# Turning attention probabilities on VectorE and by DMA instead of on TensorE

## The chip, the cores and the metric

The kernel runs on one core of a Trainium2 chip. The metric is the device time of one execution in microseconds. The core has five engines with their own instruction streams: TensorE (PE in the profile; its weight loads are PEld), VectorE (DVE), ScalarE (ACT), GpSimd (POOL) and SyncE (SP), which here only issues DMAs. Each stream runs in order, and the streams wait for each other by semaphores. Matmul results land in PSUM, everything else is in SBUF, 128 partitions wide.

## The reference

Two layers on x (8 batches x 256 tokens x 256 features, float32) with a context of 256 tokens x 192 features:

```python
x = x + xattn0(layernorm(x), ctx, mask, ...)       # 16 heads of 16
x = x + soft_moe(layernorm(x), ...)                # 8 experts, 128 slots each
x = x + xattn1(layernorm(x), ctx, ...)             # 16 heads of 64: the second attention
x = x + channel_mix(layernorm(x), ...)
```

The second attention, which alone is changed, is

```python
q = (x @ w_q).reshape(B, SQ, 16, 64)
k = (cond @ w_k).reshape(B, SKV, 16, 64)
v = (cond @ w_v).reshape(B, SKV, 16, 64)
attn = softmax(einsum('bqhd,bkhd->bhqk', q, k) * 64 ** -0.5, axis=-1)
out = einsum('bhqk,bkhd->bqhd', attn, v).reshape(B, SQ, 1024)
return out @ w_out + b_out
```

The softmax runs along the keys, so the probabilities come out with queries on the partitions. The product with v sums over keys, so it wants keys on the partitions: between the two the probabilities must be transposed.

## The kernel before

The kernel is one program in four parts; the third is the second attention. It handles 8 batches. A *step* is two of the 16 heads of one batch (t = 0 to 7), and `steps1` gives each step as a list of stages:

- stage 0, `scores`: four matmuls (L73 is the helper that records them) put the scores of two heads and 256 queries into a PSUM tile `sc` (two buffers, tag `big`). VectorE takes the row maxima `nm` (L1201). ScalarE takes four exponentials with their sums into `ex` and `z` (L1206).
- stage 1, `norm`: VectorE takes `rz`, the reciprocal of the sums (L1217); GpSimd multiplies the 128x1024 probabilities by it (L1219).
- stage 2, `transposes`: TensorE transposes the probabilities in eight 128x128 blocks (L76) into two PSUM tiles `pe` (tag `mm`, three buffers, shared with the projections); VectorE and ScalarE copy one each to `et` (L1235).
- stage 3, `values`: eight matmuls with `V` and `et` into `o`, and after every second step a ScalarE copy to `ot` (L1254).
- stage 4, `project` (after the last step of a batch): sixteen matmuls with the output weights into `po`, and VectorE adds the result to x (L1267).

Beside the steps stand the projections of later batches: `xt_piece` (normalised x, transposed: `xT`, L1121), `q_piece` (into `q`, scaled into `QT` by VectorE, L1141), `keys` (into `k`, copied to `KT` by ScalarE and VectorE, L1106 and L1107) and `values_of` (into `v`, copied to `V`, L1171 and L1172).

Two steps make a group, and there are 32 groups, four for a batch. The loop at the end of the part (L1293) sets the order of the work: in its pass n it records stage 3 of group n-3, a q piece or `xt_piece` of the next batch, stage 4 of group n-4, stages 2 and 1 of groups n-2 and n-1, a key or value projection, and stage 0 of group n. Matmuls, transposes and `rz` keep this order on their engines (`keep_in_program_order`). The passes of one batch differ: n % 4 = 0 has `xt_piece` and no q; 1 and 2 have one q piece; 3 has two q pieces and `project`. The last projections end with pass 27. The DMAs of this part load its weights (L1067 to L1080, issued from 900 to 906 us); the next DMAs that SP issues load the weights of the fourth part (L1321).

Of the kernel before, what the change touches and what calls it, by code (L numbers as in the profile page):

```python
# [8 lines left out]
F32 = mybir.dt.float32  # L9
U8 = mybir.dt.uint8  # L10
AF = mybir.ActivationFunctionType
ALU = mybir.AluOpType
AX = mybir.AxisListType

P = 128
B, S, D, C = 8, 256, 256, 192
NT = B * S // P
H = 16
HD0, HD1 = 16, 64
# [43 lines left out]
def kernel(ctx: ExitStack, tc: tile.TileContext, a: dict, out: bass.AP):  # L63
    nc = tc.nc
# [10 lines left out]
    def transpose(out, in_):  # L75
        tc.keep_in_program_order(nc.tensor.transpose(out, in_, ident))  # L76
# [7 lines left out]
    def ps_mm(name):  # L84
        return ps.tile([P, 512], F32, tag="mm", bufs=3, name=name)
# [137 lines left out]
    with ExitStack() as l0:  # L223
# [372 lines left out]
        for p in range(1, 4):  # L596
            h, b = 16 * (p - 1), 2 * p
# [160 lines left out]
        for b, plan in enumerate(  # L758
# [8 lines left out]
            for step in plan.split():  # L767
                when, _, args = step[1:].partition(".")
# [293 lines left out]
    with ExitStack() as l1:  # L1062
# [48 lines left out]
        def proj1(b):  # L1111

            to = {}

            def xt_piece():
                mv, rstd = xat_stats[b // 2]
                pt = transposed(normed(b, mv, rstd, "l1", of=4), f"x1_{b}", transpose)
                to["xT"] = p1.tile([P, 2, S], F32, tag="xT", bufs=1, name=f"xT1_{b}")  # L1120
                nc.vector.tensor_copy(to["xT"], pt)  # L1121
                for t in range(2):
                    nc.gpsimd.tensor_tensor(
                        x_sb[:, 2 * b + t, :], x_sb[:, 2 * b + t, :], bo, ALU.add
                    )

            def q_piece(t2):
                if t2 == 0:
                    to["QT"] = p1.tile([P, 8, S], F32, tag="QT", bufs=2, name=f"QT1_{b}")
                pq = ps_mm(f"q1_{b}_{t2}").rearrange("p (t n) -> p t n", t=2)  # L1130
                for i in range(2):
                    t = 2 * t2 + i
                    for c in range(2):
                        matmul(
                            pq[:, i, :],
                            lhsT=wq[:, c, t * P : (t + 1) * P],
                            rhs=to["xT"][:, c, :],
                            start=(c == 0),
                            stop=(c == 1),
                        )  # L1140
                nc.vector.tensor_scalar(  # L1141
                    to["QT"][:, 2 * t2 : 2 * t2 + 2, :], pq, HD1**-0.5, None, ALU.mult
                )

            def values_of(u):

                if u == 0:
                    to["V"] = p1.tile([P, 2, DA], F32, tag="V", bufs=2, name=f"V1_{b}")
                pv = [ps_mm(f"v1_{b}_{u}_{h}") for h in range(2)]
                t0 = S * b + u * P  # L1150
                cols = [slice(h * 512, (h + 1) * 512) for h in range(2)]
                for h in range(2):
                    matmul(
                        pv[h],
                        lhsT=ctx0T[:, t0 : t0 + P],
                        rhs=wv[:, 0, cols[h]],
                        start=True,
                        stop=False,
                    )

                def halves():
                    for h in range(2):
                        r = slice(64 * h, 64 * h + 64)
                        matmul(
                            pv[h],
                            lhsT=ctx1T[r, t0 : t0 + P],
                            rhs=wv[r, 1, cols[h]],
                            start=False,
                            stop=True,
                        )  # L1170
                    nc.scalar.copy(to["V"][:, u, cols[0]], pv[0])  # L1171
                    nc.vector.tensor_copy(to["V"][:, u, cols[1]], pv[1])  # L1172

                return halves

            qs = [[xt_piece]] + [[lambda t=t: q_piece(t) for t in ts] for ts in ((0,), (1,), (2, 3))]
            return to, qs, [lambda u=u: values_of(u) for u in range(2)]

        def steps1(b, to):
# [4 lines left out]
            for t in range(8):  # L1184
# [3 lines left out]
                def scores(t=t, tag=tag, st=st):  # L1188
                    sc = ps_big(f"sc_{tag}").rearrange("p (h q k) -> p h q k", h=2, q=2)
                    for qb in range(2):  # L1190
                        for i in range(2):
                            r = slice(64 * i, 64 * i + 64)
                            matmul(
                                sc[:, i, qb, :],
                                lhsT=to["QT"][r, t, qb * P : (qb + 1) * P],
                                rhs=to["KT"][r, t, b % 2 * S : (b % 2 + 1) * S],
                                start=True,
                                stop=True,
                            )
                    nm = stat.tile([P, 2, 2], F32, tag="nm1", bufs=4, name=f"nm_{tag}")  # L1200
                    nc.vector.tensor_reduce(nm, sc, AX.X, ALU.max, negate=True)  # L1201
                    ex = p1.tile([P, 2, 2, S], F32, tag="ex", bufs=6, name=f"ex_{tag}")
                    z = stat.tile([P, 2, 2], F32, tag="z1", bufs=6, name=f"z_{tag}")
                    for qb in range(2):
                        for i in range(2):
                            nc.scalar.activation(  # L1206
                                ex[:, i, qb, :],
                                sc[:, i, qb, :],
                                AF.Exp,
                                bias=nm[:, i, qb : qb + 1],  # L1210
                                accum_out=z[:, i, qb : qb + 1],
                            )
                    st["ex"], st["z"] = ex, z
# [9 lines left out]
                        ALU.mult,  # L1223
                    )

                def transposes(tag=tag, st=st):
                    et = p1.tile([P, 2, 2, S], F32, tag="et", bufs=4, name=f"et_{tag}")
                    for i in range(2):
                        pt = ps_mm(f"pe_{tag}_{i}").rearrange("p (c q) -> p c q", c=2)
                        for qb in range(2):  # L1230
                            for c in range(2):
                                transpose(
                                    pt[:, c, qb * P : (qb + 1) * P],
                                    st["ex"][:, i, qb, c * P : (c + 1) * P])
                        (nc.scalar.copy if i else nc.vector.tensor_copy)(et[:, i, :, :], pt)  # L1235
                    st["et"] = et

                def values(t=t, tag=tag, st=st):
                    if t == 0:
                        blk["ot"] = p1.tile([P, 8, S], F32, tag="ot", bufs=2, name=f"ot_{tag}")  # L1240
                    if t % 2 == 0:
                        blk["o"] = ps_o(f"o_{tag}").rearrange("p (t q) -> p t q", t=2)
                    for c in range(2):
                        for i in range(2):
                            h = 2 * t + i
                            matmul(
                                blk["o"][64 * i : 64 * i + 64, t % 2, :],
                                lhsT=to["V"][:, c, h * HD1 : (h + 1) * HD1],
                                rhs=st["et"][:, i, c, :],
                                start=(c == 0),  # L1250
                                stop=(c == 1),
                            )
                    if t % 2 == 1:
                        nc.scalar.copy(blk["ot"][:, t - 1 : t + 1, :], blk["o"])  # L1254

                def project(tag=tag):
# [12 lines left out]
                    )  # L1269

                steps.append(
                    [scores, norm, transposes, values] + ([project] if t == 7 else [])
                )
            return steps

# [4 lines left out]
        def stage(k, n):  # L1280
            for step in groups[n] if 0 <= n < len(groups) else ():
                if k < len(step):
                    step[k]()
# [9 lines left out]
        for n in range(len(groups) + 4):  # L1293
            b, i = n // 4 + 1, n % 4
            stage(3, n - 3)
            if b < B:
                for piece in projs[b][1][i]:
                    piece()
            stage(4, n - 4)
            stage(2, n - 2)  # L1300
            stage(1, n - 1)


            if i < 2 and n // 8 < B // 2 - 1:
                keys(n // 8 + 1, n % 8 // 4 * 2 + i)()
            elif i >= 2 and b < B:
                projs[b][2][i - 2]()()
            stage(0, n)
            if n == 20:
                ffn_stats[0] = ln_half(0, "ffn_0")  # L1310
# [159 lines left out]
```

## Time and profile before

| | |
|---|---|
| time, three runs | median 1375.35 us (1374.36 to 1376.78) |
| profiled execution | 1375.81 us, span 1373.9 us |
| mean granted TensorE clock | 0.987 |
| TensorE matmuls | busy 1326.6 us, 97% of the span |
| VectorE, ScalarE, GpSimd | busy 42%, 42%, 14% |
| second attention, first row maximum to last residual add | from 943.42 to 1315.87 us of the span |

The profile is one execution. A line of a timeline gives the start, the length, the engine, the line of the kernel, the operation and its operands; `x16` at a PE line counts matmuls and weight loads together. The length of a matmul includes the time until its result is out, so successive starts, not lengths, tell what it holds the engine for. A line of windows gives the stretch, its length, the busy time and count of PE, PEld, DVE, ACT and POOL, the granted clock, the share of DMA and GB/s.

### The profile page before, as it was taken

To read this page: it belongs to the slowest core of one execution; us is meant where nothing else is said; L and a number is where in the kernel's file an instruction comes from. 1 tells how busy PE (TensorE), PEld (TensorE's weight loads), DVE (VectorE), ACT (ScalarE), POOL (GpSimd) and SP (SyncE) were. 2 spreads that over 40 slices of the span, in tenths; PEclk is the share of its full clock that TensorE was granted. 3 is DMA by queue.
4 is the path that set the end of the run, shared out by engine and by line. 5 is a ranking of instruction groups with operands and counts; after the bars stand their busy time and mean duration, and the time that the engine had idled before them with its cause. 6 is when DMAs were issued, how large, how long until landed. Compare 5 with 4: busy or idle time off the path is not lost.

```text
span 1373.9 us, 19006 instructions
## 1 busy us (share of the span) xinstructions
PE 1326.6 (97%) x7504; PEld 961.3 (70%) x7504; DVE 575.1 (42%) x1172; ACT 578.9 (42%) x1386; POOL 194.6 (14%) x149
## 2 busy tenths in 40 slices
PE   6899999899999999999999999999999999999988
PEld 3556655468678877778767888866667667577767
DVE  5777876523330233321333110025444544554544
ACT  1445444635342254522625222204544534554643
POOL 1000001101010000100001000013332332323514
PEclk9899999999999999999999999999999999999999
DMA  8000000023133323332323325340000000000011
GB/s 250 23 2 1 1 1 1 1 96 131 65 131 131 131 76 119 130 113 83 126 69 130 131 88 173 100 126 1 1 1 1 1 1 1 1 1 1 1 31 54
DMA packets 59112, 86.84 MB, mean 63 GB/s; under 512 B 3344, under 2 KB 49040, under 8 KB 59024
## 3 DMA queue, kind: packets, MB, share of 16 engines
q1 hardware_dynamic: 57440, 84.33, 18.8%
q10 hardware_dynamic: 1584, 1.31, 0.4%
q8 instruction: 59, 0.97, 0.3%
q14 instruction: 29, 0.24, 0.1%
HBM read 83.53 MB, written 2.10 MB: 62 GB/s over the span
## 4 chain that ended last, share of the span: by engine, by line
PE 84%; ACT 6%; DVE 4%; DMA 2%; issue 2%; POOL 1%; SPq 0%; POOLq 0%; ACTq 0%; DVEq 0%
PE ph L964 16%; PE pe L980 15%; PE sc L73 8%; PE q L73 6%; PE o L73 5%; PE po L73 5%; PE k L73 5%; PE pc L1006 4%; PE v L73 4%; PE pe L76 4%; PE ln L828 3%; PE pf L910 3%; ACT ex L1206 2%; PE pf L73 1%; ACT ex L497 1%
## 5 line engine op out<-in xcount | busy, mean ns | idle before, releaser
L972 ACT ACTIVATE ht<-ph,b 128x256 f32<-128x256 f32 x256 | 119.0, 473 | 372.1 <-PE ph L964 371.7
L964 PE MATMUL ph<-slots,w 128*128 128x256 f32 x1024 | 266.8, 384 | 1.1 <-ACT ht L972 0.4
L980 PE MATMUL pe<-w,ht 128*128 128x256 f32 x1024 | 263.3, 381 | 0.0
L964 PEld LDWEIGHTS ph<-slots,w 128*128 128x128 f32 x1024 | 182.4, 189 | 54.4 <-ACT ht L972 21.7
L980 PEld LDWEIGHTS pe<-w,ht 128*128 128x128 f32 x1024 | 192.0, 190 | 29.9 <-DVE slots L989 4.2
L1219 POOL TENSOR_TENSOR ex<-ex,rz 128x1024 f32<-128x1024 f32 x64 | 120.2, 1898 | 224.4 <-DVE rz L1217 219.8
L1206 ACT ACTIVATE ex<-sc,nm 128x256 f32<-128x256 f32 x256 | 117.2, 483 | 45.8 <-DVE nm L1201 44.6
L73 PE MATMUL sc<-KT,QT 17*128 17x256 f32 (+1 forms) x1024 | 105.5, 383 | 5.7 <-DVE NM L486 4.8
L497 ACT ACTIVATE ex<-sc 128x512 f32<-128x512 f32 x128 | 74.6, 596 | 84.4 <-PE sc L73 76.6
L486 DVE TENSOR_REDUCE NM<-sc 128x2 f32<-128x512 f32 x128 | 86.7, 687 | 33.0 <-PE sc L73 28.7
L989 DVE TENSOR_TENSOR slots<-pe,b 128x512 f32<-128x512 f32 x32 | 22.1, 692 | 185.0 <-PE pe L980 185.0
L73 PEld LDWEIGHTS sc<-KT,QT 17*128 17x128 f32 (+1 forms) x1024 | 78.0, 189 | 29.0 <-issue 13.3
L73 PE MATMUL q<-xT,wq 128*128 128x256 f32 x384 | 95.4, 396 | 0.9 <-ACT V L1171 0.9
L73 PEld LDWEIGHTS q<-xT,wq 128*128 128x128 f32 x384 | 71.3, 193 | 27.0 <-issue 13.3
L888 POOL TENSOR_TENSOR es<-es,zs 128x1024 f32<-128x1024 f32 x12 | 22.7, 1893 | 445.8 <-DVE zs L887 445.8
L1201 DVE TENSOR_REDUCE nm<-sc 128x4 f32<-128x1024 f32 x64 | 75.4, 1219 | 6.5 <-PE sc L73 2.8
L73 PE MATMUL po<-wo,ot 128*128 128x256 f32 x320 | 72.6, 382 | 0.0
L76 PE MATMUL pe<-ident,ex 128*128 128x128 f32 x512 | 69.9, 278 | 0.5 <-DVE xT L1121 0.4
L73 PEld LDWEIGHTS po<-wo,ot 128*128 128x128 f32 x320 | 60.1, 190 | 11.3 <-issue 3.6
L1235 ACT COPY et<-pe 128x512 f32<-128x512 f32 x64 | 37.0, 607 | 71.9 <-PE pe L76 71.5
L76 PEld LDWEIGHTS pe<-ident,ex 128*128 128x128 f32 x512 | 56.3, 140 | 14.0 <-issue 8.0
L73 PE MATMUL o<-et,V 128*64 128x256 f32 x512 | 62.8, 385 | 0.9 <-ACT ot L1254 0.9
(186 smaller groups left out, 1642.7 us busy)
## 6 DMA issues: line engine op xcount, KB each, us to landing
w<-in_w_dram SPq DMA_DIRECT2D x64, 1024.0 KB, 6.4
b<-in_b_dram SPq DMA_DIRECT2D x32, 128.0 KB, 6.7
out_dram<-y SPq DMA_DIRECT2D x8, 256.0 KB, 2.1
x_sb<-in_x_dram SPq DMA_DIRECT2D x3, 512.0 KB, 6.1
ctx0T<-in_ctxT_dram SPq DMA_DIRECT2D x4, 256.0 KB, 6.8
ctx1T<-in_ctxT_dram SPq DMA_DIRECT2D x8, 128.0 KB, 5.9
se<-in_slots_dram SPq DMA_DIRECT2D x1, 1024.0 KB, 6.0
wq<-in_wq_dram SPq DMA_DIRECT2D x1, 1024.0 KB, 4.9
```

The source lines that it names most:

```text
L73: tc.keep_in_program_order(nc.tensor.matmul(out, lhsT=lhsT, rhs=rhs, start=start, stop=stop))
L76: tc.keep_in_program_order(nc.tensor.transpose(out, in_, ident))
L486: nc.vector.tensor_reduce(NMs[(2 * b + t // 2) % 2][:, qb, t, HD0 + 1 + 64 * i : 64 * i + 64 : 32], sc[i][:, :, 0, :], AX.X, ALU.max, nega ...
L497: nc.scalar.activation(ex[:, 2 - 2 * i : 4 - 2 * i, :], sc[1 - i][:, :, 1, :], AF.Exp)
L828: nc.tensor.matmul(pl[:, m * 512 : (m + 1) * 512], lhsT=st["xnT"][:, c, t * P : (t + 1) * P], rhs=snT[:, c, m * 512 : (m + 1) * 512], star ...
L964: nc.tensor.matmul(ph, lhsT=c_["w1"][:, c, hc * P : (hc + 1) * P], rhs=slots[e][:, c * 256 : (c + 1) * 256], start=(c == 0), stop=(c == 1),)
L972: nc.scalar.activation(ht, ph, AF.Gelu, bias=b1[:, e, hc : hc + 1])
L980: nc.tensor.matmul(c_["pe"][:, b, :], lhsT=c_["ht"][hc][:, b * SL : (b + 1) * SL], rhs=c_["w2"][:, hc, :], start=(hc == 0), stop=(hc == HI ...
L1006: nc.tensor.matmul(pc[:, :D], lhsT=CT[:, bl, e, t * P : (t + 1) * P], rhs=eos[e][:, bl, :], start=(e == 0), stop=(e == E - 1),)
L1201: nc.vector.tensor_reduce(nm, sc, AX.X, ALU.max, negate=True)
L1206: nc.scalar.activation(ex[:, i, qb, :], sc[:, i, qb, :], AF.Exp, bias=nm[:, i, qb : qb + 1], accum_out=z[:, i, qb : qb + 1],)
L1219: nc.gpsimd.tensor_tensor(ex, ex, rz.rearrange("p h q -> p (h q)").unsqueeze(2).to_broadcast([P, 4, S]), ALU.mult,)
```

## The change

The transposes leave TensorE. Stage 2 becomes `turn`: for each step one VectorE instruction transposes the probabilities in squares of 32x32 into `tk`, and after the second step of a group sixteen DMAs, issued by SP, move the squares from one quarter of the partitions to another, from `tk` to `et`. Each DMA moves 32 partitions of 2 KB. `et` and `tk` now hold a group each (two buffers), `ex` has four buffers where it had six. The matmuls of `values` read `et` in pieces of 32 elements. The scaling of `QT` goes from VectorE to ScalarE. In the loop, stage 2 is recorded for group n-1, not n-2, after the key or value projection and just ahead of stage 0 of group n; stage 1 comes ahead of stage 4. Stage 3 stays at group n-3. On VectorE the two turns of a group stand between the copy to `KT` or `V` and the row maxima of the next group.

```diff
-                nc.vector.tensor_scalar(
-                    to["QT"][:, 2 * t2 : 2 * t2 + 2, :], pq, HD1**-0.5, None, ALU.mult
+                nc.scalar.activation(
+                    to["QT"][:, 2 * t2 : 2 * t2 + 2, :], pq, AF.Copy, scale=HD1**-0.5
                 )
...
-                    ex = p1.tile([P, 2, 2, S], F32, tag="ex", bufs=6, name=f"ex_{tag}")
+                    ex = p1.tile([P, 2, 2, S], F32, tag="ex", bufs=4, name=f"ex_{tag}")
...
-                def transposes(tag=tag, st=st):
-                    et = p1.tile([P, 2, 2, S], F32, tag="et", bufs=4, name=f"et_{tag}")
-                    for i in range(2):
-                        pt = ps_mm(f"pe_{tag}_{i}").rearrange("p (c q) -> p c q", c=2)
-                        for qb in range(2):
-                            for c in range(2):
-                                transpose(
-                                    pt[:, c, qb * P : (qb + 1) * P],
-                                    st["ex"][:, i, qb, c * P : (c + 1) * P])
-                        (nc.scalar.copy if i else nc.vector.tensor_copy)(et[:, i, :, :], pt)
-                    st["et"] = et
+                def turn(t=t, tag=tag, st=st):
+                    if t % 2 == 0:
+                        blk["tk"] = p1.tile([P, 4, 2, 8, 32], F32, tag="tk", bufs=2, name=f"tk_{tag}")
+                        blk["et"] = p1.tile(
+                            [P, 4, 2, 2, 2, 2, 32], F32, tag="et", bufs=2, name=f"et_{tag}"
+                        )
+                    tk, et = blk["tk"], blk["et"]
+                    st["et"] = et[:, :, t % 2, :, :, :, :]
+                    tc.keep_in_program_order(
+                        nc.vector.transpose(
+                            tk[:, :, t % 2, :, :].rearrange("p k m x -> p m k x"),
+                            st["ex"].rearrange("p h q (c k x) -> p (h q c) k x", c=2, k=4),
+                        )
+                    )
+                    if t % 2 == 1:
+                        for k in range(4):
+                            for a in range(4):
+                                nc.sync.dma_start(
+                                    et[32 * k : 32 * k + 32, a].rearrange(
+                                        "p s h q c x -> p (s h q c x)"
+                                    ),
+                                    tk[32 * a : 32 * a + 32, k].rearrange("p s m x -> p (s m x)"),
+                                )
...
-                                rhs=st["et"][:, i, c, :],
+                                rhs=st["et"][:, :, i, :, c, :].rearrange("p a q x -> p q a x"),
...
-                    [scores, norm, transposes, values] + ([project] if t == 7 else [])
+                    [scores, norm, turn, values] + ([project] if t == 7 else [])
...
+            stage(1, n - 1)
             stage(4, n - 4)
-            stage(2, n - 2)
-            stage(1, n - 1)
...
+            stage(2, n - 1)
             stage(0, n)
```

## The prediction

> **What bounds the kernel now.** I read first the page's engine table, then the chain of waits inside the second attention, then timelines of TensorE, VectorE, ScalarE and GpSimd over one of its batches, then the DMA issues and the clock. The page says that TensorE is the bound overall; the chain over 1000 to 1100 us says that this holds in the second attention too, 89% of it being matmuls, 12.2% the transposes of the probabilities (`pe`, L76).
>
> ```profile
> PE 1326.6 (97%) x7504; PEld 961.3 (70%) x7504; DVE 575.1 (42%) x1172; ACT 578.9 (42%) x1386; POOL 194.6 (14%) x149
> by line: PE q L73 15.0%; PE po L73 13.8%; PE v L73 12.6%; PE pe L76 12.2%; PE sc L73 12.1%; PE k L73 11.6%; PE o L73 11.3%; ACT ex L1206 6.8%; DVE nm L1201 2.5%; ACT et L1235 1.3%; issue 1.1%; ACT ot L1254 0.6%; ACTq L1206 0.0%
> ```
>
> TensorE in the heaviest quarter of a batch (start, length, then line and operands). Starts give what each phase holds TensorE for: o 1.88, two q 3.55, po 6.91, pe 2.04, v 2.78, sc 1.8.
>
> ```profile
> 1051.06 1.89 PE L73 MATMUL sc<-KT,QT 64*128 64x256 f32 x16
> 1052.88 1.95 PE L73 MATMUL o<-et,V 128*64 128x256 f32 x16
> 1054.76 3.72 PE L73 MATMUL q<-xT,wq 128*128 128x256 f32 x16
> 1058.31 7.07 PE L73 MATMUL po<-wo,ot 128*128 128x256 f32 x32
> 1065.22 2.20 PE L76 MATMUL pe<-ident,ex 128*128 128x128 f32 x16
> 1067.26 1.88 PE L73 MATMUL v<-wv,ctx0T 128*128 128x512 f32 x4
> ```
>
> I call a tick one pass of the loop, that is, the work for one group (two steps, four heads); four ticks make a batch. One tick's softmax on the other engines: two row maxima on VectorE in 2.36 us, eight exponentials on ScalarE from 1043.11 to 1046.72 (3.6 us), two scalings on GpSimd in 3.74 us (in brackets: idle time before, and what ended it).
>
> ```profile
> 1041.79 2.36 DVE L1201 TENSOR_REDUCE nm<-sc 128x4 f32<-128x1024 f32 x2
> 1043.11 0.47 ACT L1206 ACTIVATE ex<-sc,nm 128x256 f32<-128x256 f32 x1 [1.61 <-DVE nm L1201]
> 1046.72 0.62 ACT L1254 COPY ot<-o 128x512 f32<-128x512 f32 x1
> 1038.52 3.74 POOL L1219 TENSOR_TENSOR ex<-ex,rz 128x1024 f32<-128x1024 f32 x2 [6.86 <-DVE rz L1217]
> ```
>
> A batch takes 49.7 us now (from one residual add, L1267, at 1015.72 to the next at 1065.42).
>
> **What goes.** Sixteen transposes per tick, 2.04 us of TensorE: 8.2 us of the 49.7, and the stall of 0.77 us that a key projection pays once a batch for PSUM held until ScalarE's copy of `et`. TensorE's own work falls to 49.7 − 8.2 − 0.8 = 40.7 us. VectorE loses an `et` copy per step (2 × 0.68) and the scaling of `QT` (0.69); ScalarE loses its `et` copies (2 × 0.59) and takes `QT` (about 0.6, as its other 128x512 copies). If TensorE stayed the bound, 32 × 2.04 = 65 us would go, less wherever others are late next.
>
> **What comes, and on which path.** (1) VectorE turns 128x1024 per step. The nearest rows: a turn of 128x512 takes 717 ns, so 1.43 at most for twice as much; a reduction over 1024 elements holds VectorE 1.17 us. I take 1.2 us, as the turn's cost per element beyond a fixed part looks like the reduction's.
>
> ```profile
> L534 DVE STREAM_TRANSPOSE zt<-o x16: 706/717/718, 63.0 to 276.1; 128x512 f32<-128x512 f32 x16
> ```
>
> The turns stand in VectorE's order behind `rz` and the KT or V copy and ahead of the next tick's row maxima. So a new loop arises: first maximum 1.2, handover 0.1, exponentials 3.6, last `rz` and scaling 2.3, second turn 1.2, handovers 0.2: 8.6 us a tick. TensorE needs 8.3 in ticks with one q, so this alone costs little; the ones without projections it slows.
>
> (2) Sixteen DMAs per tick, all issued by SP, 64 KB each. No row shows a copy from SBUF to SBUF. SP's pace does show: five loads in a row, of 256 KB or of 1 KB alike, start 0.43 to 0.51 us apart.
>
> ```profile
> 1315.21 0.38 SPq L1321 DMA_DIRECT2D sb_wrT<-in_wrT_dram  x1
> 1315.64 0.46 SPq L1321 DMA_DIRECT2D sb_wkT<-in_wkT_dram  x1
> 1316.15 0.46 SPq L1321 DMA_DIRECT2D sb_wvT<-in_wvT_dram  x1
> 1316.65 0.47 SPq L1323 DMA_DIRECT2D mu<-in_mu_r_dram  x1
> 1317.16 0.43 SPq L1324 DMA_DIRECT2D mu<-in_mu_k_dram  x1
> ```
>
> And landing, from the issues (KB, us):
>
> ```profile
> out_dram<-y SPq DMA_DIRECT2D x8, 256.0 KB, 2.1
> wo<-in_wo_dram SPq DMA_DIRECT2D x8, 32.0 KB, 2.5
> ```
>
> I take 0.47 (0.40 to 0.60) a DMA and 2.0 (1.7 to 2.5) to landing. From the end of the turns to the last landing: 15 × 0.47 + 2.0 + 0.1 = 9.15 us (7.8 to 11.6). SP has nothing else queued between 906 and 1315 us, and its 7.5 us a tick fit into a tick. The Trainium skill, DMA: Bandwidth & Descriptors, section Rules for kernel authors, says to join small transfers, since under 64 KB one pays mostly overhead: these stand at that edge. [...]
>
> (3) The wait. `values` of tick g now waits for sixteen landings, on TensorE's queue, ahead of q, po, the next k or v. VectorE's KT or V copy waits for that k or v, and the turn of tick g+2 stands behind the copy. So a round runs turn(g) → DMAs → o(g) → q, po → k or v → copy → turn(g+2), two ticks long. Round with po: 9.15 + 1.88 + 3.6 + 6.91 + 2.78 + 0.6 + 2.4 + 0.15 = 27.5. The other one of the same parity: 9.15 + 1.88 + 1.92 + 2.78 + 0.6 + 2.4 + 0.15 = 18.9. Together 46.4 a batch, above TensorE's 40.7 (the two rounds of the other parity, with k or v and at most one q, sum to some 36 and follow): it idles 5.7 us a batch, in two or three pieces just ahead of o.
>
> (4) The clock. Idle TensorE loses it:
>
> ```profile
> 214.20:217.60 3.40, 1.51 (x13) 0.94 (x10) 2.60 (x6) 2.08 (x9) 0.00 (x0) 1.00 0.00 0
> 217.60:221.00 3.40, 3.40 (x21) 2.42 (x22) 1.75 (x4) 1.94 (x5) 1.90 (x1) 0.50 0.00 0
> 221.00:224.40 3.40, 3.40 (x7) 2.01 (x8) 0.99 (x2) 0.93 (x2) 0.00 (x0) 0.50 0.00 0
> ```
>
> After 3.4 us of which TensorE (first figure) was busy 1.51, the granted clock (third from the end) is 0.50 for the next 3.4 us at least. An idle piece of 2 us or more should do this; half the clock for 3.4 us costs 1.7, and it falls on o, q and k, inside the round. With two and a half a batch: 46.4 + 4.3 = 50.7. The Trainium skill, TensorE: Matmul & The Clock Gate, Part 1, wants a whole idle window of 3.4 us; by that there would be hardly a drop and the batch would stay at 46.4, but the row above dropped at 44% busy, and I go by the row.
>
> **The sum**, against the profiled execution (1375.81 us, span 1373.9; the median is 0.5 lower). Between the first row maximum (943.42) and the last residual add (1315.87):
> - Start, three ticks: two at 8.6 against 6.4 and 9.5, one slowed clock: +3.
> - Twenty steady ticks, five batches: 250.7 now (971.41 to 1222.13). 5 × 50.7 = 253.5: +3. (At full clock 5 × 46.4 = 232: −19.)
> - The last eight ticks have few projections, so TensorE had 5.8 us in most: 74 us now (1222.13 to 1296.10). The loop of 8.6 sets five of them (43), rounds two (18.9 − 8.6 = 10.3, and 27.5 − 10.3 = 17.2), the last, with po, about 12.5, and one or two slow clocks 2.6: 85.6, +12.
> - Drain, from the last maximum to the add: 19.8 now. Then 1.3 + 3.6 + 2.3 + 1.2 + 9.15 + 1.9 + 0.75 for `ot` + 7.0 + 0.7 = 27.9, and a slow clock 1.7: +10.
>
> Together +28: 1404 us.
>
> **What is costed at nothing.** Fewer `ex`, `et` and `tk` buffers: each buffer's last reader stands before its next writer in the rounds above; the turn's extra semaphore waits cost 21 ns each on VectorE's rows, at most 5 us. The moved stage order touches GpSimd's scaling and the residual add, which have slack (GpSimd 14%). The strided moving operand of o, in pieces of 32, is in no row: nothing if it streams as now, 1.9 us a round if at half rate (+25), so it only raises the upper end. Turns of 1.43 instead of 1.2 add 0.46 a round, about +8. Loads at L1321 are issued after the last po's operands in any case.
>
> **Rivals.**
> - *The DMAs are hidden (faster).* With 0.40 a DMA and 1.7 to landing the path is 7.8, the rounds sum to 43.7, TensorE idles 3 us a batch in pieces under 1.5 us, and the clock stays up. Steady part 5 × 43.7 = 218.5 (−32), start +1, tail +6, drain +7: −18, 1358. For it: 0.43 as the first gap, 1.7 the shortest landing of `wo`. Against: all later gaps are 0.46 or more. It decides from about 8.2 us from turn to landing downwards; near 8.3 the result is near no change, above it slower.
> - *The DMAs are slower.* 0.60 a DMA (SP's pace at 902 us, in loads of 0.5 to 1 MB, was 0.64) and 2.5: 11.6; rounds +4.9 a batch: +25 steady, +10 tail and drain, on top of +28: 1439. Against: there the queue was full of megabytes.
> - *TensorE remains the bound and 65 us go* would need the landing within 4 us; the sixteen issues alone exclude it.
>
> **Chances.** Forecast 0.55, slower DMAs or operand 0.21, hidden 0.18, the strip between 0.06. The forecast's own range is 1388 to 1420. To hold 8 in 10 it reaches down into the hidden case, to 1368, and up to 1440. A measurement here tells 0.2% (2.8 us) from no change: faster 0.19, same 0.05, slower 0.76.
>
> **What would show it.** Right: DMA starts on SP 0.45 to 0.52 apart; o waiting for a DMA for 2 to 3 us in two ticks of four; granted clock near 0.93 in the second attention; batches near 51 us; ticks near 8.6 at its end. Wrong: TensorE busy above 95% there, or turns far above 1.2 us, or o longer than 1.88.

## The result and the profile after

The changed kernel takes 1447.4 us, median of four runs (1445.85 to 1449.78), against 1376.07 (1374.36 to 1377.51) for the kernel before in the same session: ratio 1.0528, 95% interval 1.0516 to 1.0541. It is slower, as forecast, but by 71 us, where the forecast said 28 and the range ended at 1440. The profiled execution took 1445.85 us, its span is 1444.1.

The engine table of the page after. TensorE has less work than before (its transposes are gone), and in a longer span its share is down by seven points:

```profile
PE 1294.4 (90%) x6992; PEld 925.7 (64%) x6992; DVE 593.7 (41%) x1140; ACT 563.2 (39%) x1354; POOL 194.6 (13%) x149
```

The chain of waits over 1000 to 1100 us, the stretch shown of before, where matmuls were 89% of it. Now SP's issues (`SPq`, L1246) and the landings lead it:

```profile
by line: SPq L1246 38.1%; PE o L73 16.5%; PE po L73 13.8%; PE q L73 10.7%; PE v L73 5.6%; DMA et<-tk 5.2%; PE sc L73 5.2%; issue 3.0%; PE k L73 2.8%
```

TensorE over a batch (start, length, line and operands, and in brackets the idle time before it with what ended it). In every second tick o waits for a landing (5.8 and 5.3 us here, 3.9 to 5.8 over the steady batches), then runs in 3.68 us instead of 1.95; a q after it takes 2.90 instead of 1.99:

```profile
1042.90 3.68 PE L73 MATMUL o<-et,V 128*64 128x256 f32 x16 [5.79 <-DMA et<-tk]
1046.51 2.90 PE L73 MATMUL q<-xT,wq 128*128 128x256 f32 x8
...
1053.84 1.95 PE L73 MATMUL o<-et,V 128*64 128x256 f32 x16
1055.72 1.99 PE L73 MATMUL q<-xT,wq 128*128 128x256 f32 x8
...
1067.50 3.68 PE L73 MATMUL o<-et,V 128*64 128x256 f32 x16 [5.29 <-DMA et<-tk]
1071.11 4.27 PE L73 MATMUL q<-xT,wq 128*128 128x256 f32 x16
1075.22 7.07 PE L73 MATMUL po<-wo,ot 128*128 128x256 f32 x32
```

What the second of these waits is made of, from the chain in order of time (start, length, what). The turns end at 1055.8; then sixteen DMAs start on SP, 0.633 us apart, and the last one lands at 1067.5: 11.7 us in all.

```profile
1055.84 0.94 SPq L1246
1056.83 0.59 SPq L1246
1057.46 0.59 SPq L1246
1058.09 0.59 SPq L1246
...
1065.06 0.59 SPq L1246
1065.76 1.75 DMA et<-tk
1067.51 3.67 PE o L73 x16
```

The new instructions by themselves (shortest, median and longest in ns; first and last start):

```profile
L1246 SPq DMA_DIRECT2D et<-tk x512: 507/589/1571, 950.3 to 1372.2; - x171
L1238 DVE STREAM_TRANSPOSE tk<-ex x64: 1201/1235/1246, 947.9 to 1359.8; 128x1024 f32<-128x1024 f32 x64
L1238 DVEq EVENT_SEMAPHORE  x120: 49/50/50, 972.6 to 1357.8; - x120
```

Their row among the page's DMA issues (KB each, median us from issue to landing):

```profile
et<-tk SPq DMA_DIRECT2D x512, 64.0 KB, 2.0
```

The clock around that wait (first figure after the length: TensorE's busy time; third from the end: granted clock). A stretch without any matmul, then half the clock:

```profile
1059.20:1062.60 3.40, 3.02 (x21) 1.85 (x20) 2.12 (x4) 2.44 (x8) 3.26 (x2) 1.00 0.42 103
1062.60:1066.00 3.40, 0.00 (x0) 0.00 (x0) 3.38 (x3) 1.05 (x5) 0.00 (x0) 0.92 0.45 109
1066.00:1069.40 3.40, 1.90 (x10) 1.28 (x12) 0.36 (x2) 2.70 (x12) 2.17 (x2) 0.50 0.40 97
```

All of the loss lies in the second attention: the last residual add (L1282) ends at 1386.71 where it ended at 1315.87, 70.8 us later, and the spans differ by 70.2. By the stretches of the forecast's sum, cut at the same row maxima:

| stretch | before, us | after, us | more | forecast | with the slower-DMA rival |
|---|---|---|---|---|---|
| start, three ticks | 28.0 | 33.9 | +5.9 | +3 | +3 |
| twenty steady ticks | 250.7 | 280.1 | +29.4 | +3 | +28 |
| last eight ticks | 74.0 | 96.9 | +22.9 | +12 | (tail and drain) |
| drain | 19.8 | 34.2 | +14.5 | +10 | +32 |

(The sum is 72.7; the first row maximum came 1.8 us earlier than before.) A batch, from one residual add to the next, takes 56.2 us on the mean of four (1025.18 to 1249.91), not 50.7.

### The profile page after: what moved, and what is told of

Its sections match the earlier page's. It is cut to its first block, busy times and chain, and to the rows that moved or that the text cites. A ratio compares the mean times of both kernels' runs of the same rounds, so it can differ in the third digit from the quotient of the medians.

```text
span 1444.1 us, 18582 instructions
## 1 busy us (share of the span) xinstructions
PE 1294.4 (90%) x6992; PEld 925.7 (64%) x6992; DVE 593.7 (41%) x1140; ACT 563.2 (39%) x1354; POOL 194.6 (13%) x149
## 4 chain that ended last, share of the span: by engine, by line
PE 71%; SPq 12%; DMA 4%; DVE 4%; ACT 4%; issue 3%; POOL 1%; POOLq 0%; DVEq 0%; ACTq 0%
PE ph L964 16%; PE pe L980 15%; SPq L1246 12%; PE sc L73 5%; PE o L73 5%; PE q L73 5%; PE po L73 5%; PE pc L1006 4%; PE k L73 3%; PE pf L910 3%; PE ln L828 3%; PE v L73 2%; DMA et<-tk 2%; PE pf L73 1%; ACT ex L497 1%
## 5 line engine op out<-in xcount | busy, mean ns | idle before, releaser
L964 PEld LDWEIGHTS ph<-slots,w 128*128 128x128 f32 x1024 | 182.3, 189 | 54.6 <-ACT ht L972 21.8
L73 PE MATMUL o<-et,V 128*64 128x256 f32 x512 | 89.1, 508 | 100.4 <-DMA et<-tk 91.0
L73 PEld LDWEIGHTS o<-et,V 128*64 128x64 f32 x512 | 49.6, 182 | 134.6 <-issue 84.1
L73 PE MATMUL sc<-KT,QT 17*128 17x256 f32 (+1 forms) x1024 | 110.2, 390 | 15.0 <-ACT ex L1206 8.9
L73 PE MATMUL q<-xT,wq 128*128 128x256 f32 x384 | 99.4, 409 | 0.9 <-ACT V L1171 0.9
L73 PEld LDWEIGHTS q<-xT,wq 128*128 128x128 f32 x384 | 74.6, 203 | 31.3 <-issue 13.6
L1238 DVE STREAM_TRANSPOSE tk<-ex 128x1024 f32<-128x1024 f32 x64 | 77.2, 1229 | 11.0 <-POOL ex L1219 10.5
L73 PEld LDWEIGHTS po<-wo,ot 128*128 128x128 f32 x320 | 60.5, 191 | 11.8 <-issue 3.9
L1006 PE MATMUL pc<-slots,CT 128*128 128x256 f32 x256 | 57.5, 379 | 0.0
```

The source lines that it names most:

```text
L73: tc.keep_in_program_order(nc.tensor.matmul(out, lhsT=lhsT, rhs=rhs, start=start, stop=stop))
L964: nc.tensor.matmul(ph, lhsT=c_["w1"][:, c, hc * P : (hc + 1) * P], rhs=slots[e][:, c * 256 : (c + 1) * 256], start=(c == 0), stop=(c == 1),)
L1006: nc.tensor.matmul(pc[:, :D], lhsT=CT[:, bl, e, t * P : (t + 1) * P], rhs=eos[e][:, bl, :], start=(e == 0), stop=(e == E - 1),)
L1238: nc.vector.transpose(tk[:, :, t % 2, :, :].rearrange("p k m x -> p m k x"), st["ex"].rearrange("p h q (c k x) -> p (h q c) k x", c=2, k=4),)
```

## The experiments

Theory after the result: the forecast's round (turn, sixteen DMAs, o, q and po, k or v, the copy, the turn two ticks on) and its clock term are right, and the one term that is off is SP's pace, 0.633 us a DMA instead of 0.47. The path from the turns to the last landing is then 15 x 0.633 + 2.0 + 0.1 = 11.6 us. Rivals: something else in the round grew (the strided operand of o, semaphore waits, VectorE's order), or the DMA engines, not the issuing queue, set the pace. The kernel before took 1374.79 us in the session of four of the kernels below (twelve DMAs, copy behind the turns, one tick deeper, TensorE kept busy), 1374.31 in that of the other three; the two probes have one profile and one time each. Two of the expectations put a batch of the changed kernel at 54.6 us; its trace has 56.2.

| kernel | us | ratio to before (95%) |
|---|---|---|
| twelve DMAs, four copies | 1395.0 | 1.0137 (1.0115 to 1.0160) |
| four DMAs from GpSimd | 1408.0 | 1.0248 (1.0214 to 1.0282) |
| copy behind the turns | 1408.9 | 1.0249 (1.0234 to 1.0264) |
| TensorE kept busy | 1429.0 | 1.0400 (1.0379 to 1.0421) |
| one tick deeper | 1358.9 | 0.9886 (0.9870 to 0.9902) |
| deeper, four DMAs from GpSimd | 1351.1 | 0.9832 (0.9817 to 0.9847) |
| deeper, twelve DMAs | 1343.2 | 0.9774 (0.9760 to 0.9789) |

**1. Twelve DMAs instead of sixteen.** The four squares that stay in their quarter of the partitions are copied by GpSimd, so that the path on SP is about as short as the forecast had it.

```diff
-                                nc.sync.dma_start(
+                                (nc.gpsimd.tensor_copy if a == k else nc.sync.dma_start)(
```

> Theory: the sum's form was right and only SP's pace was mis-sized (0.633 us a DMA measured, 0.47 forecast). The four squares that stay in their quarter are copied by GpSimd, SP issues 12 DMAs, so turn to last landing is 11 x 0.633 + 2.0 + 0.1 = 9.1 us, the 9.15 of the forecast: 1404 us, 1400 to 1412. Rival: the excess over the forecast comes from elsewhere (a strided operand of o, the clock, semaphore waits), and a shorter issue leaves the time within 10 us of 1447.

Measured: 1395.0 us, 5 us below the range that the theory expected. A batch takes 49.1 us on the mean of four (forecast for its own path: 50.7), and the waits of o for landings fall from 91.0 us (after) to 54.5, from the views of TensorE's waits between 940 and 1390 us (who waited for whom: us in total, times, longest), first of after, then of this kernel:

```profile
PE o L73 <- DMA et<-tk: 91.0, 16, 11.1
```

```profile
PE o L73 <- DMA et<-tk: 54.5, 20, 8.3
```

With the path that the forecast had assumed (11 x 0.633 + 2.0 + 0.1 = 9.1 us) the kernel lands 9 us below the forecast's 1404. Cut as in the table above, its stretches are longer than before by 2.7, -3.6, 14.2 and 9.5 us, where the forecast had +3, +3, +12 and +10: so the rest of the sum holds within 7 us a stretch. Four DMAs fewer are worth 52 us, though, where the forecast's sums for the two paths (1404 and the rival's 1439) differ by 35. A shorter path is not all that they change: twelve DMAs hold SP for 7.6 us a tick, sixteen for 10.1.

**2. The same four fewer on SP, but as DMAs.** GpSimd issues the four into the last quarter.

```diff
-                                nc.sync.dma_start(
+                                (nc.gpsimd if k == 3 else nc.sync).dma_start(
```

> The changed kernel with the four of a turn's sixteen DMAs whose destination is the last quarter issued by GpSimd, the other twelve by SP. Theory (the pace belongs to the issuing queue): SP's chain falls to 11 x 0.633 + 2.0 + 0.1 = 9.1 us, as where GpSimd copied four squares (1395): 1390 to 1408, with GpSimd's issue costs and the scalings behind them in its order as the uncertain part; SP's starts stay 0.63 us apart. Rival (the DMA engines behind all queues set the pace): the starts of all sixteen still spread over 9.5 us and the time stays within 1 per cent of the changed kernel, 1435 to 1455.

Measured: 1408.0 us, at the upper edge of what the theory expected. SP's DMAs keep their 0.589 us each, and those on GpSimd's queue are issued in 0.496 us each beside them:

```profile
L1246 SPq DMA_DIRECT2D et<-tk x384: 507/589/1458, 949.0 to 1322.8; - x192
...
L1246 POOL DMA_DIRECT2D et<-tk x128: 496/496/662, 949.3 to 1317.0; - x128
```

All 512 DMAs still run, and 39 us of the 71 come back: the pace belongs to the issuing queue, not to the engines that carry the data. The Trainium skill, DMA: Bandwidth & Descriptors, section Rules for kernel authors, says that spreading DMAs over issuing engines brings no bandwidth and only saves issue time; these rows show the saved issue time, which is what was short here, and no run here measures the bandwidth.

In the second attention itself (first row maximum to last residual add, in the profiled executions) this kernel is as good as the one with copies: 397.3 us against 395.2, and 445.1 in the changed kernel. It loses time at the very end of the program, where an instruction that drains GpSimd takes 11.8 us; in the kernel with copies (second line) it takes 1.4:

```profile
L1481 POOLq DRAIN  x3: 34/102/11836, 1391.1 to 1403.4; - x3
```

```profile
L1481 POOLq DRAIN  x3: 34/78/1362, 1392.7 to 1396.6; - x3
```

**3. The key or value projection behind the turns.** Stage 2 is recorded ahead of the projection, so that the turns no longer wait for the copy to `KT` or `V`.

```diff
+            stage(2, n - 1)
             if i < 2 and n // 8 < B // 2 - 1:
                 keys(n // 8 + 1, n % 8 // 4 * 2 + i)()
             elif i >= 2 and b < B:
                 projs[b][2][i - 2]()()
-            stage(2, n - 1)
             stage(0, n)
```

> The key or value projection is recorded after the turns, so the turns no longer stand behind the KT or V copy on VectorE. Theory: the two-tick round turn, DMAs, o, q, k or v, copy, turn is what sets the batch; without the copy in it the ring is three ticks long (4 x (11.6 + o 1.9 + q 1.9 + k 2.8 + copy 0.6 + maxima to turn 8.6) plus po in three of four, by three: about 48 to 49.5 us a batch instead of 54.6), 1447 - 30 = 1415 us, 1408 to 1425. Rival: SP's issue rate (16 x 0.633 = 10.1 us a tick) or TensorE's order alone sets it, and the place of the copy changes nothing: within 5 us of 1447.

Measured: 1408.9 us, at the lower end of the range that the theory expected. A batch takes 49.2 us (mean of four, 1020.06 to 1217.06), 6.9 less than after. The forecast's terms for k or v (2.78) and the copy (0.6) make 3.4 a round and 6.8 a batch. So the place of the copy matters: it was a link of the round. That the two sums meet does not show what the round is now. The expectation's three-tick sum, added up from its own terms, makes about 43 us, not 48 to 49.5. And in the tick with po the turns still come late: on VectorE they stand behind the residual add, which waits for po (add at 1070.29, turns at 1070.89).

**4. One tick more between turn and o.** Stages 3 and 4 move one tick later, and key and value projections change places so that keys and values are still there in time.

```diff
-        for n in range(len(groups) + 4):
+        for n in range(len(groups) + 5):
...
-            stage(3, n - 3)
+            stage(3, n - 4)
...
-            stage(4, n - 4)
+            stage(4, n - 5)
...
-            if i < 2 and n // 8 < B // 2 - 1:
-                keys(n // 8 + 1, n % 8 // 4 * 2 + i)()
-            elif i >= 2 and b < B:
-                projs[b][2][i - 2]()()
+            if i >= 2 and n // 8 < B // 2 - 1:
+                keys(n // 8 + 1, n % 8 // 4 * 2 + i - 2)()
+            elif i < 2 and 1 < b <= B:
+                projs[b - 1][2][i]()()
```

> Stage 3 is recorded for group n-4 and stage 4 for n-5, so the DMAs have one more tick; key and value projections swap places. Theory: the wait for the landings leaves TensorE's path, TensorE (40.7 us a batch) and SP (40.5) set the batch: 40.5 to 43 us against 49.7 before, the last ticks go at SP's 10.1, the drain is some 12 us longer: 25 us below before, 1350, 1342 to 1362. Rival: once SP issues back to back it is the bound with landings and buffer waits added, no gain over before: 1376 or above.

Measured: 1358.9 us, 1.1% below before and within the range that was expected. The stretch from 1000 to 1200 us, first in the changed kernel, then in this one (TensorE's busy time of 200 us, and third from the end the granted clock):

```profile
1000.00:1200.00 200.00, 161.26 (x812) 105.96 (x812) 89.05 (x125) 77.47 (x269) 55.30 (x32) 0.90 0.30 74
```

```profile
1000.00:1200.00 200.00, 193.80 (x1091) 129.59 (x1089) 124.14 (x173) 102.98 (x361) 72.21 (x41) 1.00 0.41 101
```

Nothing was made cheaper; the same sixteen DMAs now have a tick more of TensorE's work beside them. Of the waits of o that the view gives to landings, 20.7 us are left, all but 0.9 of them in the last ticks and the drain. But SP has come close to being the bound: it issues 304 DMAs in these 200 us, 192 us at 0.633 each, and its issues still lead the chain of waits over the stretch:

```profile
by line: SPq L1246 47.9%; PE q L73 9.3%; PE o L73 8.6%; PE sc L73 7.4%; PE k L73 6.9%; PE po L73 6.9%; issue 6.0%; PE v L73 5.6%; DMA et<-tk 1.0%; PE pt_x L76 0.6%
```

A batch takes 42.0 us (mean of four, 1013.47 to 1181.66); the forecast had put TensorE's own work at 40.7, and SP needs 64 x 0.633 = 40.5.

**5. TensorE kept busy while it waits.** Matmuls whose result nobody reads stand ahead of o: six, two and three of them in three ticks of four. They shorten neither the path nor the round; they only keep TensorE from idling.

```diff
+            if 3 <= n < 32 and n % 4:
+                idle = ps_mm(f"idle_{n}")
+                for _ in range((0, 6, 2, 3)[n % 4]):
+                    matmul(idle, lhsT=wk[:, 0, 0:P], rhs=wk[:, 0, 0:512], start=True, stop=True)
             stage(3, n - 3)
```

> TensorE fills its waits ahead of o with useless matmuls (6, 2 and 3 of 128x512 in the ticks that wait), whose results nobody reads. Theory: the granted clock of 0.5 after a wait lengthens o and q inside the round (3.68 and 2.9 us against 1.88 and 1.9 in the same trace); with TensorE kept busy the clock stays at 1.0 in the steady batches, a batch falls from 54.6 to some 52 us, total 1433, 1428 to 1440. Rival: the slow clock falls into time that is waited anyway, and the extra matmuls only cost: 1447 or above.

Measured: 1429.0 us, 18 us below the changed kernel although it has more to do. The granted clock from 1000 to 1200 us is 1.00, and a batch takes 52.3 us (mean of four, 1020.52 to 1229.52): the clock was at least 3.9 us of the 56.2, as the extra matmuls by themselves can only lengthen a batch. The forecast had 4.3.

**6. The two best together.** The deeper order with the four copies on GpSimd: the edits of 4 and 1.

> The changed kernel with one tick more between turn and o (as in the run that did this alone, 1359) and with the four diagonal squares copied by GpSimd, so that SP issues twelve DMAs (as in the run that did that alone, 1395). Theory (with the deeper order the steady part is TensorE's and the wait shows only in the last eight ticks and the drain): the shorter path saves 2.5 us in the drain and about 1 to 2 us in each of the last ticks, and the last waits of the steady part: 1342 to 1354. Rival (the deeper order has already hidden everything that SP's pace could cost): 1356 to 1362, as with sixteen.

Measured: 1343.2 us, 31 us below before, the best version found here. Its first three batches take 42.2 us (mean, 1010.01 to 1136.64), the next 45.0 and the one after it 38.6: in the steady part four DMAs fewer bring nothing (twenty ticks take 209.2 us, with sixteen DMAs 204.7). They help behind it, where the last eight ticks take 72.9 us instead of 79.1 and the drain 36.7 instead of 47.9. Its last waits for landings, from the timeline of TensorE, are the two of the drain:

```profile
1262.64 3.62 PE L73 MATMUL o<-et,V 128*64 128x256 f32 x16 [2.90 <-DMA et<-tk]
1270.71 3.68 PE L73 MATMUL o<-et,V 128*64 128x256 f32 x16 [4.45 <-DMA et<-tk]
```

**7. The deeper order with four DMAs from GpSimd.** The edits of 4 and 2.

> The deeper order, with the four DMAs into the last quarter issued by GpSimd instead of copied by it. Theory (the pace is the queue's, and GpSimd's issue costs no more than SP's): as with the four copies, 1342 to 1356. Rival (GpSimd pays above 1 us an issue, and the next tick's scaling stands behind four of them): 1360 to 1385.

Measured: 1351.1 us, within what the theory expected: GpSimd's issue costs 0.5 us, not above 1. The 8 us above the version with copies are not in the second attention, which takes 342.7 us here and 344.9 there; they lie at the end of the program, where GpSimd's drain takes 11.8 us again, and 1.4 with copies.

**8. What SP's pace depends on.** The kernel before with series of sixteen extra DMAs on SP (`pdst` and `psrc` are tiles made for this, with 2 KB a partition).

```diff
+                if kind == "p32_2k":
+                    nc.sync.dma_start(pdst[q, m, :], psrc[o, :])
+                elif kind == "p32_64":
+                    nc.sync.dma_start(pdst[q, m, 0:16], psrc[o, 0:16])
...
+                elif kind == "hbm32_2k":
+                    nc.sync.dma_start(pdst[q, m, :], a["wq1"][q, 0:512])
...
+                elif kind == "p64_2k":
...
+                elif kind == "p128_2k":
+                    nc.sync.dma_start(pdst[:, m, :], psrc)
```

> The kernel before, with eight series of sixteen extra DMAs issued by SP in its second attention, each series of one shape, into two tiles that nothing reads; nothing else changes and the output is the reference's. The changed kernel's DMAs (SBUF to SBUF, 32 partitions x 2 KB) start 0.633 us apart where five loads of the kernel before started 0.43 to 0.51 us apart. Theory 1: the 32 rows on few partitions are what costs: then 32 x 2 KB from SBUF starts 0.63 us apart, 32 x 2 KB from HBM also 0.60 to 0.65, 16 rows less or the same, and 128 x 2 KB 0.43 to 0.51. Theory 2: a source in SBUF is what costs: then all series from SBUF start about 0.63 us apart whatever their rows and bytes (32 x 64 bytes, 64 x 2 KB and 128 x 2 KB too), and the one from HBM 0.43 to 0.51. Theory 3: the DMA's wait for semaphores in the changed kernel is what costs: then 32 x 2 KB here, without waits on other engines, starts 0.43 to 0.51 us apart.

Measured, in the order: 32 rows of 2 KB, 32 of 64 bytes, 32 of 2 x 1 KB, 32 of 2 KB from HBM, 16 of 2 KB, 64 of 2 KB, 128 of 2 KB (lengths in ns: shortest, median, longest):

```profile
L1286 SPq DMA_DIRECT2D pdst<-psrc x32: 507/589/1036, 908.2 to 1006.1; - x32
L1288 SPq DMA_DIRECT2D pdst<-psrc x16: 588/589/590, 924.7 to 934.2; - x16
L1290 SPq DMA_DIRECT2D pdst<-psrc x16: 585/595/1856, 934.8 to 945.9; - x16
L1295 SPq DMA_DIRECT2D pdst<-in_wq_dram x16: 366/419/528, 946.6 to 953.6; - x16
L1297 SPq DMA_DIRECT2D pdst<-psrc x16: 572/588/1067, 954.1 to 964.0; - x16
L1300 SPq DMA_DIRECT2D pdst<-psrc x16: 462/588/599, 964.7 to 974.6; - x16
L1302 SPq DMA_DIRECT2D pdst<-psrc x16: 464/465/496, 975.6 to 994.4; - x16
```

The 0.633 us is SP's price for this form of DMA also without any wait on another engine: sixteen of 64 bytes a row start from 924.7 to 934.2, 9.5 / 15 = 0.633 apart. So theory 3 falls, and for 32 rows the bytes do not matter. Theory 1 falls too: 32 rows from HBM take 0.419, so it is not the few rows. Theory 2 misses on one series, the 128 rows from SBUF with 0.465. But these start 1.25 us apart (975.6 to 994.4), so SP paused between them, and whether 0.465 can be compared with the others is not shown.

**9. A second probe of the same.** Seven series with 256 bytes a row, source and destination on the same partitions.

```diff
+                if kind == 32:
+                    nc.sync.dma_start(d[0:32], psrc[0:32, m])
...
+                elif kind == 120:
+                    nc.sync.dma_start(d[0:120], psrc[0:120, m])
+                elif kind == 128:
+                    nc.sync.dma_start(d, psrc[:, m])
+                elif kind == "hbm64":
+                    nc.sync.dma_start(d[64:128], a["wq1"][64:128, m])
+                elif kind == "hbm128":
+                    nc.sync.dma_start(d, a["wq1"][0:128, m])
```

> The kernel before with seven more series of sixteen extra DMAs on SP, each of 256 bytes a row into a tile that nothing reads; source and destination lie on the same partitions. The first probe found 0.633 us from start to start for 32, 64 and 16 rows from SBUF, whatever the bytes, 0.467 for 32 rows from HBM, and an issue of 0.465 us for 128 rows from SBUF. Theory 1 (from SBUF, fewer than all 128 partitions cost more): 32, 64, 96 and 120 rows start 0.63 us apart, 128 rows about 0.51, and both series from HBM 0.47 to 0.51. Theory 2 (the shift from one partition to another costs, and the 128-row series had none): all five series from SBUF start 0.47 to 0.51 us apart. Theory 3 (bytes or rows in number set it): starts change step by step from 32 to 128 rows.

Measured, in the order 32, 64, 96, 120 and 128 rows from SBUF, then 64 and 128 rows from HBM:

```profile
L1285 SPq DMA_DIRECT2D pdst<-psrc x16: 507/588/1512, 908.4 to 923.3; - x16
L1287 SPq DMA_DIRECT2D pdst<-psrc x16: 591/594/596, 924.0 to 933.5; - x16
L1289 SPq DMA_DIRECT2D pdst<-psrc x16: 592/593/1104, 934.2 to 944.3; - x16
L1291 SPq DMA_DIRECT2D pdst<-psrc x16: 791/792/932, 944.9 to 957.6; - x16
L1293 SPq DMA_DIRECT2D pdst<-psrc x16: 573/600/1802, 958.5 to 969.3; - x16
L1295 SPq DMA_DIRECT2D pdst<-in_wq_dram x16: 594/595/602, 969.9 to 979.5; - x16
L1297 SPq DMA_DIRECT2D pdst<-in_wq_dram x16: 332/430/1622, 980.2 to 988.9; - x16
```

All three theories miss. The shift between partitions is out (32 rows on the same partitions cost 0.588 as well), but 128 rows from SBUF now take 0.600 and 64 rows from HBM 0.595. What sets SP's price between 0.42 and 0.60 us is left open. In the two probes every series from SBUF cost 0.588 or more, but for the 128 rows of 2 KB; of the three from HBM two cost 0.419 and 0.430 and one 0.595. Rows of 64 bytes and of 2 KB cost the same at 32 rows; whether that holds at 128 rows (0.600 with 256 bytes, 0.465 with 2 KB) these series do not show. The one series outside these bounds, 120 rows in 0.792, has a count that sixteen does not divide; the Trainium skill, DMA: Bandwidth & Descriptors, section Why a DMA increments its semaphore by 16 and not by 1, says that a DMA is spread over the largest number of engines up to 16 that divides the outermost sizes, which would make 15 of 120 and 16 of all the others. The page names no price for it.

## Why the prediction was right or wrong

- **The step that failed is in (2): "I take 0.47 (0.40 to 0.60) a DMA".** It measured 0.633, above the upper bound itself (the five rows that it is taken from average 0.49). The path became 11.6 us instead of 9.15, as with the rival of slower DMAs, which had it from 0.60 and a landing of 2.5; the landing was 2.0, as taken. That rival's sum was 1439. The step took the pace of five loads of 256 KB or of 1 KB from HBM and argued from their bytes; the form of these DMAs was in none of them. In the trace of before, the second attention's first loads (256 KB to 1 MB), named in the rival and set aside because "there the queue was full of megabytes", had the right pace, 0.64; the first probe shows SP at 0.633 with 64 bytes a row.
- **"Its 7.5 us a tick fit into a tick" fell with it.** Sixteen DMAs hold SP for 10.1 us, more than the 8.6 us of a tick without projections. In the last ticks of the changed kernel the queue falls ever further behind: the turns of four ticks end at 1306.76, 1315.28, 1323.80 and 1332.31, 8.5 us apart, and their first DMAs start at 1306.82, 1316.95, 1327.08 and 1337.41, the last one 5.1 us late. It shows in the drain too: the next to last tick's turns end at 1352.55 and hold SP until 1362.7, so the last tick's DMAs, ready at 1361.1, start late, and their last one starts at 1372.2 (the L1246 row above). From the timelines of TensorE and VectorE:

```profile
1359.82 1.25 DVE L1238 STREAM_TRANSPOSE tk<-ex 128x1024 f32<-128x1024 f32 x1 [0.61 <-POOL ex L1219]
```

```profile
1364.46 3.68 PE L73 MATMUL o<-et,V 128*64 128x256 f32 x16 [11.12 <-DMA et<-tk]
1374.60 3.68 PE L73 MATMUL o<-et,V 128*64 128x256 f32 x16 [6.45 <-DMA et<-tk]
```

  From the last turn to o it is 13.5 us, not 9.15, and 1.9 more than the rival's 11.6. This queueing was in no step, and in the rival neither, whose sum stays 5 us short of the last eight ticks and the drain (32 against 37.4), 3 of the start and 1 of the steady ticks; how much of these SP's queue makes beyond the 1.9 was not measured by itself and stays open.
- **(3), the round: right.** Its sum for a path of 11.6 us is 46.4 + 4.9 = 51.3 us a batch at full clock; with the clock kept up a batch took 52.3. With the turns ahead of the copy a batch lost 6.9 us (6.8 by the terms), and with a path of 9.1 us the batch was 49.1 where the forecast said 50.7. The waits came in two ticks of four, as put, but 4 to 6 us long instead of 2 to 3; that the residual add, too, stands between po and a turn was not in the round.
- **(4), the clock: right in size.** Forecast 4.3 us a batch, measured at least 3.9; the mean granted clock of the second attention is 0.87 in the changed kernel (from 941.65 to 1386.71), not near 0.93, as the waits are longer. The waits became so long that they hold a whole idle stretch of 3.4 us, so in the changed kernel the rule of the Trainium skill (TensorE: Matmul & The Clock Gate, Part 1) and the forecast's row say the same. In the kernel with four DMAs on GpSimd they part: there o took 3.68 us after a wait of 2.92, shorter than any idle window of the rule. There the row decided rightly (third from the end of a line of windows: the granted clock):

```profile
1078.94 3.68 PE L73 MATMUL o<-et,V 128*64 128x256 f32 x16 [2.92 <-DMA et<-tk]
```

```profile
1075.60:1079.00 3.40, 0.48 (x6) 0.11 (x5) 2.06 (x3) 0.19 (x1) 2.94 (x3) 0.85 0.38 92
1079.00:1082.40 3.40, 3.40 (x16) 1.81 (x16) 3.06 (x3) 1.38 (x7) 2.00 (x4) 0.50 0.30 69
```

  But "an idle piece of 2 us or more should do this" does not hold each time: in the same kernel o took 1.95 us after a wait of 2.04 (at 1051.55).

- **(1), the turn: right**, 1.235 us against 1.2, and ticks without projections do run at 8.5 us where no wait stands in them (row maxima at 1306.68, 1315.20 and 1323.72 in the changed kernel).
- **Costed at nothing.** The strided operand of o: right, at full clock o takes 1.95 us as before. The semaphore waits of the turns: 50 ns each, not 21, so 120 x 50 = 6.0 us on VectorE where the text said 5 at most; what they cost the round was not measured by itself.
- **TensorE as the bound** was not out of reach of the change, only of the order it came in: with a tick more between turn and o, batches came to 42.0 us with all sixteen DMAs, 1.3 above TensorE's own work as forecast.

## What to carry to other kernels

When a change puts many DMAs on one queue, the price that counts is that queue's time per issue for just this form of DMA, times their number, both against the path and against the length of a tick; take it from a row with the same rows and the same source, and where there is none, let the bound reach up to the slowest pace of a series anywhere in the trace. A wait that a round of dependencies cannot hide can be hidden by distance: one tick more between the issue and its reader turned 5% slower into 1% faster. After that the queue itself is close to the bound, and fewer DMAs added another 1%, in the ticks with little other work. Where TensorE waits a few microseconds in every round, add the half clock that can follow to the price of the wait.

## What the runs showed of the hardware

- SP needed 0.42 to 0.60 us for an issue (medians of the probes' series; 0.79 for 120 rows) and some 0.04 between two: 32 rows of 64 bytes and 32 rows of 2 KB from SBUF both take 0.589. GpSimd issued the DMAs of 32 rows of 2 KB in 0.496 us, with a landing of 2.3 us instead of 2.0; in the two kernels where it did, its drain at the end of the program took 11.8 us instead of 1.4.
- A copy of 64 KB from SBUF to SBUF lands 2.0 us after its issue, as one of 64 KB from HBM does in the first probe.
- VectorE's turn of 128x1024 in fp32, in squares of 32x32, takes 1.235 us, and each of the semaphore waits ahead of the turns 50 ns. GpSimd copies 32x512 in 0.607 us (kernel with twelve DMAs).
- TensorE's clock can be halved after a wait of 2.9 us too (o in 3.68 us instead of 1.95), not only after one that holds a whole idle stretch of 3.4 us; after a wait of 2.0 us in the same kernel it was not (1.95 us).
